# Four transformer layers on one core: token attention repacked into blocks of six heads

## The chip, the core and the metric

One core of a Trainium2 chip. The metric is device time in microseconds of the whole kernel. All tensors are float32. The engines are TensorE (PE in the profile, with its weight loads shown apart as PEld), VectorE (DVE), ScalarE (ACT), GpSimd (POOL) and SyncE (SP), which here does nothing but issue DMAs, in order.

## What is computed

The input is x of 4 sequences x 512 tokens x 288 channels and a condition vector per sequence. Four layers follow one another. Each has this shape (cut from the reference):

```python
shift1, scale1, gate1, shift2, scale2, gate2 = split(silu(c) @ w_ada + b_ada, 6)
h = layernorm(x) * (1 + scale1) + shift1
q, k, v = split_heads(h @ w_qkv + b_qkv)                 # 16 heads of 18
o = softmax(q @ k.T / sqrt(18)) @ v                      # over the 512 tokens of a sequence
x = x + gate1 * (o @ w_proj + b_proj)
h = layernorm(x) * (1 + scale2) + shift2
x = x + gate2 * mlp(h)                                   # 288 -> 1152 -> 288, gelu
```

Layers 0, 1 and 3 attend over tokens. Layer 2 attends, within each token, over its 16 heads. Layer 0's MLP is a mixture of four experts with the top two chosen per token.

## The kernel before, in words

The kernel is a single instruction stream per engine, whose order is made by a small scheduler at build time. The main loop of a stage emits its own matmuls and calls `gap(us)` between them (L139). Each call advances a counter `now` by one and lets `fill` (L120) emit pieces of waiting tasks into the gap: `products` (pieces with matmuls, as many as fit into `us` of estimated cost), `lanes` (DVE, ACT and POOL pieces), `loads` and `spreads` (DMAs). A task has a due gap, keys that must be marked ready, and a generator whose yields are estimated costs. A task that isn't due is taken only while the gap's allowance lasts; a due one is taken always. What a piece overshoots its allowance by is forgotten at the next gap. A mark (`mark`, L99) counts gaps, not time: the true waits are semaphores that the framework places between the instructions.

**Token attention (`attention`, L529).** A sequence b has four units of four heads; a unit takes four steps, one for each 128 rows of scores, so that a layer has 64 steps and six more ahead of them. In a step, `scores` (L648, called twice) multiplies, for the unit six steps ahead, queries by keys, whose row maxima DVE takes (L668), and for the present unit keys by queries, to which ACT applies exp (L661). `sum_values` (L683) then multiplies the exps of the step before by the values, which have a column of ones, so that the denominators come out as one more row. A head has 18 numbers and one more (`HO` is 19): the query's 19th holds the row maximum, the key's is -1, so that the maximum is subtracted within the matmul.

In the gaps of these steps lie, for each sequence:

- `chunks` (L493): the normed tokens are transposed and modulated, in three chunks of 96 channels. The third has a row of ones (97 rows), which brings the biases in.
- `queries_keys` (L578): 608 columns (4 units x 2 x 4 heads x 19) in five blocks of at most 128, with three matmuls of 512 columns for each (L562), copied by ACT (L587) into a ring of three tiles `qc`.
- `values` (L566): four tiles of tokens, three matmuls of 288 columns each (L562).
- `spread` (L592): one DMA per head and per query or key, two where a head straddles two blocks, moves 19 rows from `qc` to the unit's tile `qk`, where a head starts at row 0, 32, 64 or 96 (L606). These DMAs are issued by SP, and partly by ACT for the first unit.
- `set_maxima` (L672): four transposes (L676) of a unit's maxima, a copy by ACT (L678) and four DMAs (L680) into the 19th row of the queries.
- `denominators` and `normalise` (L701, L714): for each unit four transposes (L704) of the copied outputs (L698), a reciprocal (L706), a copy by POOL that repeats them over the head's 32 rows (L710), four transposes back (L717) and a multiplication by DVE (L720). All this stays within the engines.
- `project` (L724): four tiles, four matmuls of 288 columns (L727) each over a unit's 128 rows, most of which are padding; then the gate (L522) and the addition to x (L523).

`load_attention` (L228) loads the padded query and key weights of a layer: per unit, six DMAs of the weights (L248) and two of the biases (L252). `scale_queries` (L279) scales the query weights on POOL.

**Other stages.** Layer 0's expert MLP (`expert_block`, L1436) runs 19 blocks of 256 tokens. SP loads each block's tokens (L1382) and weights (L1397 to L1404), while the products of layer 1's first sequence, with their `spread` DMAs, already lie in its gaps. Its first four blocks are listed when two sequences are done; the others need all four. In layer 1 the MLP of sequence 0 is emitted within the attention's step 48 (`early_mlp`, L1813). Layer 2's attention over heads (`attention_over_heads`, L819) is a chain of DVE and POOL work beside layer 1's last MLPs; it writes its outputs to memory (`scratch`, L898) and reads them back (L902) through SP. Layer 3 is like the others, with a plain MLP at the end.

Of the kernel before, what the change touches and what calls it, by code (L numbers as in the profile page):

```python
# [16 lines left out]
NH, HD = 16, 18  # L17
# [23 lines left out]
UQ = 2 * HG * HO  # L41
NQ = NG * UQ
NQB = -(-NQ // P)
# [15 lines left out]
def tile_dit_blocks(ctx: ExitStack, tc: tile.TileContext, x_in, cond_t, sel_den, sel_b, w_gate, layers, out):  # L59
# [28 lines left out]
    flow = {"now": 0, "turn": 0, "others": (6, 7), "credit": 0.0, "rate": 0.0}  # L88
# [31 lines left out]
    def fill(where, started, us):  # L120

        while True:
            if not started:
                item = take(where, us <= 0)
                if item is None:
                    return
                started.append(item)
            if us <= 0 and started[0][0] > flow["now"]:
                return
# [5 lines left out]
            if took is WAIT:  # L135
                return
            us -= took

    def gap(us):  # L139
# [3 lines left out]
        fill(products, open_product, 0.0 if wanted else us)  # L143
# [57 lines left out]
    selb = const.tile([P, B, P], F32, name="selb")  # L201
# [9 lines left out]
    mxs = [const.tile([P, TB, HG], F32, name=f"mx{i}") for i in range(2)]  # L211


    spreads_of = [const.tile([P, 2, S], F32, name=f"qk{i}") for i in range(4)]

    def clear():
        for t in spreads_of:
            nc.gpsimd.memset(t, 0.0)
        mark("cleared")
        yield 0.5  # L220
# [5 lines left out]
    w_att = {l: {} for l in range(n_layers)}  # L226

    def load_attention(l):  # L228

        w, t = layers[l], w_att[l]  # L230

        wqk = wpool.tile([P, NK, NQ + C], F32, tag="wqk", name=f"wqk{l}")
        if l == OVER_HEADS:
            wqk = t["wqkv"] = wqk[:, :, : 3 * C]
            nc.sync.dma_start(wqk[:KP], w["wqkv"].rearrange("(k p) f -> p k f", p=KP))
            nc.sync.dma_start(wqk[KP : KP + 1, NK - 1, :], w["bqkv"])
        else:

            src = w["wqk"].rearrange("(k p) s (h d) -> p k s h d", p=KP, d=HP)
            bias = w["bqk"].rearrange("(o j d) s g -> o s g j d", o=1, d=HP)  # L240
            t["wqk"] = wqk[:, :, :NQ]
            wv = t["wv"] = wqk[:, :, NQ:]

            def load_unit(g, queue):
                for s in range(2):
                    at = slice(g * UQ + s * HG * HO, g * UQ + (s + 1) * HG * HO)
                    for k in range(NK):
                        queue.dma_start(  # L248
                            wqk[:KP, k, at].rearrange("p (j d) -> p j d", d=HO),
                            src[:, k, s, g * HG : (g + 1) * HG, :HO],  # L250
                        )
                    queue.dma_start(  # L252
                        wqk[KP : KP + 1, NK - 1, at].rearrange("p (j d) -> p j d", d=HO), bias[:, s, g, :, :HO]
                    )
                if g == 0:
                    queue.dma_start(wv[:KP], w["wv"].rearrange("(k p) f -> p k f", p=KP))
                    queue.dma_start(wv[KP : KP + 1, NK - 1, :], w["bv"])
                mark(("loaded", l, g), 6)

            t["load unit"] = load_unit  # L260
            if l > 0:
                for g in range(NG):
                    load_unit(g, nc.sync)
# [3 lines left out]
    def load_projection(l):  # L267
        w, t = layers[l], w_att[l]
        wp = wpool.tile([P, NG, C], F32, tag="wp", name=f"wp{l}")
        t["wp"] = wp  # L270
        if l == OVER_HEADS:
            nc.sync.dma_start(wp[:KP, :NK, :], w["wp"].rearrange("(k p) f -> p k f", p=KP))
            nc.sync.dma_start(wp[KP : KP + 1, NK - 1, :], w["bp"])
        else:
            nc.sync.dma_start(wp, w["wp"].rearrange("(g p) f -> p g f", p=P))
# [3 lines left out]
    def scale_queries(l, g):  # L279

        at = slice(g * UQ, g * UQ + HG * HO)
        for k in range(NK):
            q = w_att[l]["wqk"][: KP + (1 if k == NK - 1 else 0), k, at]
            nc.gpsimd.tensor_scalar_mul(q, q, SCALE)  # L284
        mark(("weights", l, g))
# [62 lines left out]
    def mod_product(l, half, kinds):  # L348
# [13 lines left out]
        for kind in kinds:  # L362
            at = slice(kind * HP, kind * HP + B)
            nc.vector.tensor_tensor(row[at, :C], pr[at, :C], bada[at, :], ALU.add)
            if kind < 2 and half == 1 and l:
# [8 lines left out]
    def modulation(l, half, kinds=range(3)):  # L374
# [6 lines left out]
        if half == 0:  # L381
# [5 lines left out]
        if half == 0:  # L387
# [1553 lines left out]
```

## Time and profile before

| what | value |
|---|---|
| time, median of 3 runs | 2488.81 us (2487.93 to 2495.96) |
| time of the profiled execution | 2477.4 us, of which the span of its instructions is 2475.6 us |
| token attention, layers 0, 1, 3 | about 45 to 472, 916 to 1354, 1936 to 2304 us of the span |
| expert MLP of layer 0 | about 472 to 916 us |
| attention over heads beside layer 1's MLPs | about 1354 to 1761 us |
| MLP of layer 2; MLP of layer 3 | about 1761 to 1936; 2304 to 2476 us |
| PE clock granted, mean | 0.941 of full |
| DMAs `qk<-qc` and `qk<-maxima` on SP | 417 and 192 |

The page gives busy time by engine, then the span in 40 slices of 61.9 us, each digit a tenth. A float32 matmul stands in the records as two instructions, a transpose as one; so the page's x384 for L727 are 192 matmuls (a few records are missing). A matmul's end is modelled, and one overlaps the next, so that busy times of lines add up to somewhat more than the time they take. Idle time of an engine is put down to what released it.

### The profile page before, as it was taken

The numbers are of one execution on the slowest core, as the hardware profiler recorded it, in microseconds if no ns is written. First come the engines' busy times: TensorE is split into PE (matmuls) and PEld (weight loads), VectorE is DVE, ScalarE is ACT, GpSimd is POOL, SyncE is SP. The second block draws the span as 40 slices with busy tenths as digits, with TensorE's granted clock in tenths as the row PEclk, the third lists the DMA queues.
The fourth block names the chain that finished last, engine by engine and source line by source line (L and its number), as shares of the span: only waits on it lengthen the run. The fifth ranks groups of instructions, "written<-read, shape, count | busy, mean of one in ns | idle before, by whom it ended". The sixth has DMA issues, their size and how long they took to land. (4 is left out here: it accounts for less than half of the span.)

```text
span 2475.6 us, 30149 instructions
## 1 busy us (share of the span) xinstructions
PE 2278.4 (92%) x11188; PEld 1211.7 (49%) x11188; DVE 1087.1 (44%) x1955; ACT 833.6 (34%) x1233; POOL 527.8 (21%) x544
## 2 busy tenths in 40 slices
PE   5999999799998999999998999778599999999998
PEld 2333333367775763333353676455467433333455
DVE  3556656240021124655434768989210445555100
ACT  1344444232222223444335233323223244444311
POOL 2000022130121110110010357778721000001000
PEclk7899999899999998999999999788799799999999
DMA  3211120366644540000000001111210100000000
GB/s 81 97 58 39 51 86 29 96 201 183 188 136 149 181 141 20 12 16 14 26 21 1 22 5 45 21 17 17 24 55 1 28 16 16 14 13 7 1 20 20
DMA packets 163033, 134.23 MB, mean 54 GB/s; under 512 B 81365, under 2 KB 146725, under 8 KB 162886
## 3 DMA queue, kind: packets, MB, share of 16 engines
q1 hardware_dynamic: 159520, 122.39, 17.0%
q0 software_dynamic: 3072, 9.44, 1.2%
q8 instruction: 89, 1.46, 0.2%
q14 instruction: 58, 0.48, 0.1%
q10 hardware_dynamic: 294, 0.47, 0.1%
HBM read 90.67 MB, written 26.25 MB: 47 GB/s over the span
## 5 line engine op out<-in xcount | busy, mean ns | idle before, releaser
L668 DVE TENSOR_REDUCE mx<-banks 128x1 f32<-128x512 f32 x696 | 448.0, 686 | 356.8 <-PE banks L616 356.2
L616 PE MATMUL banks<-qk 32*128 32x512 f32 x3072 | 537.1, 669 | 24.6 <-DMA qk<-qc 13.4
L661 ACT ACTIVATE ex<-banks 128x1024 f32<-128x1024 f32 x348 | 356.4, 1024 | 495.2 <-PE banks L616 493.0
L616 PEld LDWEIGHTS banks<-qk 32*128 32x128 f32 x3072 | 174.5, 191 | 238.4 <-DVE mx L668 97.2
L873 POOL TENSOR_TENSOR pv<-hs,qk 128x1152 f32<-128x1152 f32 x64 | 203.8, 3195 | 50.6 <-DVE ho L885 35.7
L690 PE MATMUL banks<-ex,va 128*32 128x512 f32 x1536 | 210.5, 619 | 0.0
L562 PE MATMUL banks<-ht,wqk 96*128 96x512 f32 (+1 forms) x360 | 189.7, 634 | 1.4 <-POOL wqk L284 0.8
L1472 PE MATMUL banks<-w_b,hid_b 128*128 128x288 f32 x684 | 187.8, 417 | 0.0
L1660 PE MATMUL banks<-ht,w 128*128 128x256 f32 x504 | 135.9, 406 | 36.0 <-ACT hid L1671 35.5
L1452 PE MATMUL banks<-block,w_b 128*128 128x256 f32 x684 | 164.4, 385 | 2.7 <-DMA w_b<-in_w 2.0
L710 POOL COPY rec<-r 128x512 f32<-128x512 f32 x48 | 29.5, 615 | 635.9 <-DVE r L706 562.2
L1682 PE MATMUL banks<-w,hid 128*128 128x288 f32 x504 | 155.6, 446 | 0.0
L1464 ACT ACTIVATE hid_b<-banks,b_b 128x256 f32<-128x256 f32 x171 | 68.7, 473 | 240.3 <-PE banks L1458 167.5
L1472 PEld LDWEIGHTS banks<-w_b,hid_b 128*128 128x128 f32 x684 | 124.0, 190 | 51.5 <-issue 23.1
L1452 PEld LDWEIGHTS banks<-block,w_b 128*128 128x128 f32 x684 | 128.8, 193 | 28.4 <-issue 7.8
L1660 PEld LDWEIGHTS banks<-ht,w 128*128 128x128 f32 x504 | 99.8, 203 | 60.4 <-ACT hid L1671 40.1
L727 PE MATMUL banks<-wp,ot 128*128 128x288 f32 x384 | 117.4, 431 | 5.9 <-DVE upd_a L522 3.5
L1682 PEld LDWEIGHTS banks<-w,hid 128*128 128x128 f32 x504 | 95.7, 202 | 48.0 <-issue 26.6
L523 POOL TENSOR_TENSOR x<-x,upd_a 128x288 f32<-128x288 f32 x48 | 38.0, 791 | 360.5 <-DVE upd_a L522 337.9
L562 PEld LDWEIGHTS banks<-ht,wqk 96*128 96x128 f32 (+1 forms) x360 | 61.2, 191 | 101.7 <-issue 87.8
L727 PEld LDWEIGHTS banks<-wp,ot 128*128 128x128 f32 x384 | 67.6, 192 | 74.9 <-issue 51.2
L690 PEld LDWEIGHTS banks<-ex,va 128*32 128x32 f32 x1536 | 30.9, 109 | 149.4 <-issue 147.7
(224 smaller groups left out, 2577.8 us busy)
## 6 DMA issues: line engine op xcount, KB each, us to landing
w_b<-in_w SPq DMA_DIRECT2D x57, 432.0 KB
w_b<-in_w SPq DMA_DIRECT2D x57, 384.0 KB
qk<-qc SPq DMA_DIRECT2D x327, 38.0 KB
wa<-in_wada SPq DMA_DIRECT2D x7, 864.0 KB
block<-x_mem SPq DMA_DIRECT2D x19, 288.0 KB
y_mem<-y_b SPq DMA_DIRECT2D x19, 288.0 KB
x_mem<-zeros SPq DMA_DIRECT2D x7, 768.0 KB
y_mem<-zeros SPq DMA_DIRECT2D x7, 768.0 KB
```

The source lines that it names most:

```text
L562: nc.tensor.matmul(to, st(rows, k), mv(rows, k), start=k == 0, stop=k == NK - 1)
L616: nc.tensor.matmul(to, qk[u][r, of, c * P : (c + 1) * P], qk[u][r, 1 - of, :], start=True, stop=True)
L661: nc.scalar.activation(e, WEIGHTS, AF.Exp)
L668: nc.vector.tensor_reduce(mxs[mu % 2][:, mc, h : h + 1], pm[j], AX.X, ALU.max)
L690: nc.tensor.matmul(SUMS[j * HP : (j + 1) * HP, :], vas[0][:, c, at : at + HP], ex[step, j // 2][:, j % 2, :], start=c == 0, stop=c == TB - 1,)
L727: nc.tensor.matmul(pp, done[b * NG + g][:, t * P : (t + 1) * P], w["wp"][:, g, :], start=g == 0, stop=g == NG - 1)
L873: nc.gpsimd.tensor_tensor(prod, sc[i][:, hs, :].unsqueeze(2).to_broadcast([P, GH, HD, NH]), qkv[i][:, 1].rearrange("p h d -> p d h").unsqu ...
L1452: nc.tensor.matmul(banks[:, UP + j, :BT], w1[:, k, j * P : (j + 1) * P], hx[i][:, k, :], start=k == 0, stop=False)
L1464: nc.scalar.activation(t, banks[:, UP + j, :BT], AF.Gelu_apprx_tanh, bias=b1[:, f : f + 1])
L1472: nc.tensor.matmul(banks[:, PY + t, :C], hid[j][:, t * P : (t + 1) * P], w2[:, j, :], start=f == 0, stop=f == NF - 1)
L1660: nc.tensor.matmul(banks[:, UP + j, :BT], full[:, k, (f % 3) * P : (f % 3 + 1) * P], h[:, k, s], start=k == 0, stop=False,)
L1682: nc.tensor.matmul(banks[:, PY + t, :C], hf[:, t * P : (t + 1) * P], w["w2"][f // 3][:, f % 3, :], start=False, stop=f == NF - 1,)
```

## The change

Layer 2 keeps its layout. In layers 0, 1 and 3:

- **Blocks.** Queries and keys are made in three blocks of six, six and four heads. A block fills two PSUM banks, one with queries and one with keys. Channels are cut as 128, 128 and 32; the 32 are stored repeatedly, at rows 0, 32 and 64, so that the last matmuls of two products can use different rows of the array. Biases leave the matmul: ACT adds them (and scales the queries) in the copy out of PSUM, DVE adds the values' bias. `scale_queries` becomes `scale_biases`, three small POOL instructions.
- **Spread.** One DMA per head carries queries and keys.
- **Maxima.** One transpose instead of four.
- **Outputs.** `gather_heads` packs a unit's outputs by five DMAs from SP into three tiles of 108, 90 and 90 rows, with the denominators beside them. The reciprocals are taken once for a sequence (eight transposes in all), written to memory with each row repeated 18 times, read back, and multiplied in by POOL. `project` takes three matmuls for a tile. The ring `ot` goes from seven tiles to four.
- **Loads.** Weights come in six DMAs for the layer, biases and projection rows are first packed in memory and then read; `selb` is no longer loaded. The zeros of the expert memory are written through POOL's queue.
- **Account.** Within the steps, what a gap's pieces overshoot or leave of their allowance is carried to the next (between -4 and 2), and the second allowance of a step goes from 1.0 to 1.4.
- The hidden tiles of the MLPs move from `ot` to `ex` (layer 1's and 2's halves stay in `ot`, two to a tile); `early_mlp` goes by two instead of three.

```diff
-UQ = 2 * HG * HO
+BLOCKS = ((0, 6), (6, 12), (12, 16))
+HEADS = ((0, 6), (6, 11), (11, 16))
...
         wanted = any(item[1] for item in chain)
-        fill(products, open_product, 0.0 if wanted else us)
+        if flow["even"]:
+            us = min(flow["room"] + us, 2.0)
+        flow["room"] = max(fill(products, open_product, 0.0 if wanted else us), -4.0)
...
+        for s in range(2):
+            for k in range(KF):
+                nc.sync.dma_start(
+                    full[:, k, s, :].rearrange("p (h d) -> p h d", d=HO), src[k * P : (k + 1) * P, s, :, :HO]
+                )
+            nc.sync.dma_start(
+                rest[s * RC : (s + 1) * RC].rearrange("p (h d) -> p h d", d=HO), src[KF * P :, s, :, :HO]
+            )
+        for g in range(NG):
+            nc.sync.dma_start(
+                packed_biases[l, g], w["bqk"].rearrange("(j d) s g -> g j d s", d=HP)[g, :, :HO, :]
+            )
+        rows = packed_biases[l].rearrange("g j d s -> (g j d) s")
+        for i, (h0, h1) in enumerate(BLOCKS):
+            nc.sync.dma_start(bqk[: (h1 - h0) * HO, :, i], rows[h0 * HO : h1 * HO, :])
...
-        PACE = (0.3, 1.0)
+        PACE = (0.3, 1.4)
...
+            to = [other()[:n, :] for _ in range(2)]
+            for s in range(2):
+                for k in range(KF):
+                    nc.tensor.matmul(to[s], w["full"][:, k, s, at], h[:, k, :], start=k == 0, stop=False)
+                    yield 0.86
+            for s in range(2):
+                r = slice(s * RC, (s + 1) * RC)
+                nc.tensor.matmul(to[s], w["rest"][r, at], h[r, KF, :], start=False, stop=True)
+            t = packed[b, i] = work.tile([P, 2, S], F32, tag="qc", bufs=2, name=f"qc_{l}_{b}_{i}")
+            for s in range(2):
+                nc.scalar.activation(
+                    t[:n, s, :], to[s], AF.Identity, bias=w["bqk"][:n, s, i : i + 1], scale=SCALE if s == 0 else 1.0
+                )
...
-                        queue = nc.scalar if u == 0 and j >= HG // 2 else nc.sync
-                        queue.dma_start(t[to : to + n, s, :], packed[b, m][r : r + n, :])
+                nc.sync.dma_start(t[j * HP : j * HP + HO], packed[b, i][r : r + HO])
...
-            for c in range(TB):
-                nc.tensor.transpose(pm[:HG, c * P : (c + 1) * P], mxs[u % 2][:, c], ident)
+            nc.tensor.transpose(pm[:n, :P], mxs[u % 2].rearrange("p j c -> p (j c)"), ident)
...
+        def gather_heads(u):
...
+            at = KP + 1 + g * HG
+            nc.sync.dma_start(last[at : at + HG, :], done[u][ONE::HP, :])
+            for j in range(HG):
+                k = [i for i in range(NK) if HEADS[i][0] <= g * HG + j < HEADS[i][1]][0]
+                at = (g * HG + j - HEADS[k][0]) * HD
+                nc.sync.dma_start(oc[b][k][at : at + HD, :], done[u][j * HP : j * HP + HD, :])
...
+        def normalise(b):
+            rows = dram.tile([NH, HD, S], F32, tag="rec", name=f"rec_rows_{l}_{b}")
+            nc.sync.dma_start(rows, rec[b][1 : 1 + NH, :].unsqueeze(1).to_broadcast([NH, HD, S]))
+            rows = rows.rearrange("h d s -> (h d) s")
...
+                    nc.sync.dma_start(room[k], rows[r0:r1, :])
+                for _ in range(3):
+                    yield WAIT
+                for k in ks:
...
+                    nc.gpsimd.tensor_tensor(oc[b][k][:n, :], oc[b][k][:n, :], room[k], ALU.mult)
+            mark(("outputs", l, b), 3)
...
-                    products, at_step(last if b + 1 == B else last + (7 if l == 0 else 11) + t),
-                    [("outputs", l, b * NG + g) for g in range(NG)] + [("gate", l, 0), ("projection", l)], project(b, t),
+                    products, at_step(last + 8 + 2 * t), [("outputs", l, b), ("gate", l, 0), ("projection", l)], project(b, t)
```

## The prediction

> **What bounds the kernel now.** I read the page's busy times and slices first, then the stretches of single stages, then TensorE's groups within layer 3's attention, its waits over the whole run, and SP's timeline where TensorE waited for a DMA.
>
> ```profile
> span 2475.6 us, 30149 instructions
> ...
> PE   5999999799998999999998999778599999999998
> ...
> PEclk7899999899999998999999999788799799999999
> ```
>
> TensorE is busy in nine tenths of most slices, and the clock falls where it was idle. The stretches (PE, PEld, DVE, ACT, POOL busy, clock) of layer 3's attention, of the attention over heads, and of one piece of the expert MLP:
>
> ```profile
> 2050.00:2100.00 50.00, 49.39 (x290) 17.61 (x292) 26.25 (x45) 22.06 (x25) 4.09 (x6) 1.00 0.05 17
> ...
> 1350.00:1750.00 400.00, 346.49 (x1428) 244.05 (x1424) 314.96 (x337) 120.42 (x228) 260.59 (x158) 0.88 0.10 20
> 735.00:785.00 50.00, 38.96 (x163) 26.93 (x162) 10.33 (x23) 8.20 (x20) 14.56 (x14) 0.90 0.43 131
> ```
>
> Token attention is TensorE's: 49.39 of 50 us, with DVE at 53%. The attention over heads is a chain of DVE (315 of 400 us) and POOL, so TensorE work saved there gives nothing. TensorE's groups from 2000 to 2290 us, where 13 units (3.25 sequences) pass:
>
> ```profile
> L616 PE MATMUL banks<-qk 32*128 32x512 f32 x824 | 125.6, 639 | 0.2 <-ACT ex L643 0.2
> L690 PE MATMUL banks<-ex,va 128*32 128x512 f32 x416 | 55.4, 605 | 0.0
> L562 PE MATMUL banks<-ht,wqk 96*128 96x512 f32 (+3 forms) x72 | 37.5, 625 | 0.0
> L727 PE MATMUL banks<-wp,ot 128*128 128x288 f32 x96 | 31.2, 435 | 1.3 <-DVE upd_a L522 1.2
> L562 PE MATMUL banks<-wqk,ht 96*128 96x288 f32 (+1 forms) x72 | 22.7, 433 | 1.2 <-DVE va L572 1.2
> L676 PE MATMUL banks<-ident,mx 128*4 128x128 f32 x52 | 8.7, 272 | 3.2 <-DVE mx L668 3.2
> L717 PE MATMUL banks<-ident,rec 128*128 128x128 f32 x52 | 8.3, 282 | 0.0
> L704 PE MATMUL banks<-ident,ot 128*128 128x128 f32 x52 | 8.2, 281 | 2.2 <-ACT ot L698 2.2
> ```
>
> Idle before these is 8 us of 290. With 5.6 us for the transposes of L508 they sum to 303 us, so a busy us stands for 0.93 us of time (282/303). TensorE's DMA waits over the run, and SP's queue at one of them:
>
> ```profile
> PE banks L1425 <- DMA block<-x_mem: 20.6, 3, 9.0
> PE banks L915 <- DMA rows<-scratch: 18.7, 1, 18.7
> ...
> PE banks L616 <- DMA qk<-qc: 13.4, 2, 12.4
> ```
>
> ```profile
> 735.30 19.89 SPq L606 DMA_DIRECT2D qk<-qc  x18
> ...
> 758.19 11.59 SPq L606 DMA_DIRECT2D qk<-qc  x9
> ```
>
> SP issues one after the other; 27 spread DMAs at 0.6 to 1.3 us hold back an expert block's tokens and weights, and TensorE stands at 759 us.
>
> **The change part by part.** *TensorE, for a sequence.* From the groups: a query or key matmul takes 37.5/36 = 1.04 us, a values one 0.63, a projection one 0.65, a transpose 0.16 to 0.17.
>
> Before: queries and keys 15 x 1.04 = 15.6; values 12 x 0.63 = 7.6; projection 16 x 0.65 = 10.4; maxima 16 x 0.17 = 2.7; denominators and back 32 x 0.16 = 5.1. Sum 41.4.
>
> After: queries and keys 12 x 1.04 = 12.5, and three pairs of 32-row remainders. Nearest row: L1604 does three such remainders at once, 17.0 us for 15 triples, 1.1 us; three pairs 3.3. Values 8 x 0.63 and two pairs at 0.7 (L1667's pairs of 256 columns take 0.63 from their start to the next matmul's): 6.4. Projection 12 x 0.65 = 7.8; maxima 4 x 0.17 = 0.7; reciprocals 8 x 0.16 = 1.3. Sum 32.0.
>
> The difference is 9.4 busy us, 8.7 us of time; for 12 sequences 105 us. Could it be less? The Trainium skill (Perfetto Trace Analysis, Identifying the Most-Contended Engine) says that matmul busy share doesn't show how full TensorE is, and to go by weight-load share: here 17.6/50 = 35%. By that rule TensorE has room and the saving is near 0. But in this window something follows each matmul at once, and neither DVE nor ACT is over 55%; I go by the gaps, not by the modelled ends. A step is 5.6 us now and would be 5.1. The exp chain sets a floor: two score rounds of 1.1 us, each followed by an exp of 1.02 before its banks are free, 4.4 us a step. Steps that get few pieces come near it and lose part of the gain. I take 80%: **-84 us** (bounds -52 and -105).
>
> *DVE and ACT.* DVE loses 48 multiplications of 0.69 us, ACT gets six biased copies of 0.77 (row L509) for five of 0.59 a sequence: both are off the path, hidden by TensorE; uncovered, ACT's would cost 12 x 1.7 = 20 us. POOL gets three multiplications of some 1.25 us (between L523's 0.79 for 288 columns and L1694's 1.40 for 576) a sequence and loses four copies of 0.61: hidden, at 7% busy.
>
> *SP.* A unit's spread falls from about nine DMAs to four, the gather adds five, the maxima stay four: 13 either way, about 8 of 22 us. But what is moved matters. In the expert MLP the spreads become 12 instead of 27: the 11 us of idle around 759 and half of the 10 us at half clock behind it should go. Loads of a layer shrink from 34 DMAs to some 17, so that L915 (18.7 us behind 23 us of loads) gains 6 to 8, and layer 1's load before the expert MLP about 4. The start (12.4 us for the first `qk<-qc`) may gain 3, less what the packed biases' two trips take. **-25 us** (-10 to -35).
>
> *New waits.* (a) Reciprocals go through memory: SP writes 590 KB, waits for it to land, then reads. The row: `rows<-scratch`, the same size, took 4.4 us from issue (1794.08) to the transposes it releases (1798.50): 8.8 for both ways. The skill (DMA: Bandwidth & Descriptors, Anatomy of one DMA) gives 2.0 us fixed plus bytes at 436 GB/s, 6.7 for both, and says that a wait on memory can be surprisingly long. I take the row; no one needs the projection for some steps, so TensorE waits 0. What is queued behind SP in that time is a `set_maxima` or a `spread`: 0 to 4 us a sequence. (b) `set_maxima` may be emitted a gap later. Now the ACT copy L678 starts 6.3 to 14 us, mostly over 10, before the copy L698 of the unit before, and that stands about 2 us behind the scores that read the row: 4.3 to 12 us are there. Four issues of 0.54 (L680) and the same page's 2.0 us of landing need 4.2. A gap is 2.6 us; the tight units would stall 1 to 2 us. Both: **+8** (0 to 40). (c) A pair holds both free banks (6 and 7), so a pair right behind another waits for ACT, up to 1.5 us, five a sequence: **+8** (0 to 30). (d) Layer 0's last sequence: its outputs come some 30 gaps of 1.2 us behind the attention instead of 13 us. Block 4 of the experts was loaded at 554 us and used at 576, so that 18 us were spare: **+11** (0 to 25) with the slow clock behind the stall. Layer 3's last sequence has 111 us of MLPs ahead of it, and needs about 90: 0 (to 15). The account, the rings, POOL's zeros and the early MLP by two (two more remainder groups at some 1 us): 0 to 2, I take 0; bounds -5 and +5.
>
> Sum: -84 - 25 + 27 = -82 on 2477.4, the profiled execution's own time (span 2475.6): 2395. The median of the runs is 0.46% above that execution: **2406 us**.
>
> **The rivals.**
>
> *All of it arrives.* The account keeps all steps even: -105 - 35 + 10 = -130, 2347, as a median 2358. For it: idle is so small now. Against: the exp floor.
>
> *Half is eaten.* Late maxima and paired banks cost what the upper bounds allow, the exp floor takes half: -52 - 10 + 40 = -22, as a median 2466.
>
> *SP becomes the pacemaker.* The normalisation, now free of DMAs, hangs on 20 gathers a sequence; SP stands at each new sequence until the tiles `oc` are free, and the four maxima DMAs of each unit stand behind. If the first weights of each of 48 units then wait 3.5 us, that is 168 us, over twice the saving: +86, as a median 2575. It decides from 82/48 = 1.7 us a unit. For it: the expert MLP shows just this blocking, and a 3.3 us gap at 996 us was followed by 10 us at half clock. Against: `qk<-maxima` cost TensorE 1.0 us in all before, with as many DMAs.
>
> **How the numbers follow.** The main case 0.45 (2375 to 2445), all arrives 0.22, half eaten 0.13, SP 0.20. About 0.3% is what a measurement of this kernel can tell from no change. Half eaten gives 0.08 to faster and 0.05 to the same: faster 0.75, same 0.05, slower 0.20. The range, 2335 to 2515, holds all but the SP case and a thin tail below.
>
> **What would show it.** The three attentions should be 25 to 35 us shorter each, with L727 at x288 and L676 at x48. The stand at 759 should be gone, L915's wait shorter, a new stand at the experts' block 4. If TensorE shows waits for the maxima's DMA at many units, or slices of attention below 9, the SP case holds. I am wrong also if the steps stay at 5.6 us though TensorE has less to do.

## The result, and the profile after

The changed kernel takes 2566.81 us (median of 4 runs, 2562.18 to 2571.13) beside 2488.37 us before: a ratio of 1.033, 95% interval 1.030 to 1.0359. It is slower. I had predicted 2406 us, in a range of 2335 to 2515. The profiled execution:

```profile
span 2565.3 us, 28976 instructions
...
PE   6899989589996999989999999869669999999998
...
PEclk9799999789998997998999989879789899999999
```

The page counts 10732 matmul records on PE where there were 11188, and yet more slices lie below 9. By stage (columns: PE, PEld, DVE, ACT, POOL busy, clock granted, DMA share, GB/s), for the start to attention 0's end, the experts, attention 1, attention over heads with MLPs, attention 3. Before:

```profile
45.20:445.90 400.70, 385.44 (x2156) 141.77 (x2156) 232.58 (x492) 171.73 (x209) 42.70 (x69) 0.96 0.17 58
445.90:916.00 470.10, 443.27 (x2104) 318.23 (x2096) 81.19 (x253) 111.90 (x246) 72.05 (x95) 0.96 0.52 159
916.00:1348.30 432.30, 409.59 (x2192) 163.44 (x2194) 212.29 (x389) 176.38 (x207) 42.49 (x56) 0.95 0.08 24
1348.30:1935.80 587.50, 505.58 (x2062) 351.13 (x2056) 331.48 (x377) 172.21 (x326) 310.19 (x221) 0.88 0.12 25
1935.80:2301.00 365.20, 351.55 (x2006) 130.95 (x2006) 199.77 (x357) 165.82 (x192) 27.29 (x40) 0.96 0.04 11
```

After:

```profile
50.60:475.00 424.40, 390.79 (x1996) 145.92 (x1998) 224.97 (x477) 171.27 (x217) 56.61 (x83) 0.94 0.21 67
475.00:980.30 505.30, 446.41 (x2112) 320.00 (x2104) 80.04 (x252) 114.20 (x251) 73.20 (x92) 0.93 0.50 152
980.30:1434.30 454.00, 423.52 (x2032) 162.63 (x2032) 200.92 (x362) 174.57 (x212) 47.01 (x54) 0.92 0.13 36
1434.30:2024.50 590.20, 501.35 (x2070) 344.14 (x2066) 327.76 (x376) 174.86 (x330) 310.75 (x215) 0.89 0.13 27
2024.50:2389.80 365.30, 351.81 (x1844) 133.37 (x1844) 188.32 (x330) 162.13 (x195) 32.03 (x38) 0.95 0.10 27
```

The loss is +24 us in attention 0, +35 in the experts, +22 in attention 1, +5 at the start, and nothing in attention 3. But attention 3 has 162 records fewer and didn't gain either; PE is as *busy* as before. The granted clock is lower as well: at 0.95 in place of 0.92 attention 1 would take 454.0 x 0.92/0.95 = 440 us, by an estimate that lets its whole time go with the clock.

These stages are from one profile each. Attention 0 took 401 us at a clock of 0.96 here, and 416 us at 0.93 in v1_before_later (below), which is the same program up to 430 us. So of the +24 up to 15 us may be the clock of that one execution. (The changed kernel's attention 0 took 425 us in two profiles; attention 3 takes 365 to 367 us in the profiles of before, v1 and y4.) TensorE's groups in 290 us of layer 3's attention (to be read beside those of before):

```profile
L635 PE MATMUL banks<-qk 32*128 32x512 f32 x810 | 156.7, 641 | 3.8 <-DMA qk<-tops 3.8
L712 PE MATMUL banks<-ex,va 128*32 128x512 f32 x408 | 55.5, 617 | 0.0
L603 PE MATMUL banks<-ht,wqk 128*114 128x512 f32 (+1 forms) x56 | 30.8, 654 | 0.7 <-DVE upd_a L538 0.6
L791 PE MATMUL banks<-wp,oc 108*128 108x288 f32 (+2 forms) x72 | 21.0, 424 | 0.0
L580 PE MATMUL banks<-wqk,ht 128*128 128x288 f32 x48 | 13.5, 421 | 0.0
...
L695 PE MATMUL banks<-ident,mx 128*16 128x128 f32 x13 | 3.6, 277 | 4.1 <-DVE va L586 2.5 <-ACT qc L610 0.8 <-ACT ht L525 0.8
```

The products shrank as worked out. The scores, untouched by the change, went from 125.6 us for 824 records to 156.7 for 810, with the same mean of one. That is the main reading of this case: a wait hidden in busy time. For all three attentions, the time from each matmul's start to the next one's, added up by kind (us; "sums" are the exps times the values, "other products" all else that TensorE does there):

| kernel | scores | sums | other products | the three attentions |
|---|---|---|---|---|
| before | 515 | 204 | 481 | 1198 |
| after | 657 | 196 | 391 | 1244 |
| after, rows cut at 16 (below) | 627 | 194 | 374 | 1196 |

The other products and sums fell by 98 us, and the scores took 142 more. TensorE's waits:

```profile
PE banks L748 <- DMA oc<-ot: 30.0, 3, 29.3
PE banks L635 <- DMA qk<-tops: 23.7, 13, 7.0
PE banks L973 <- DMA rows<-scratch: 22.9, 2, 20.7
...
PE banks L1483 <- DMA block<-x_mem: 14.6, 2, 14.1
...
PE banks L1510 <- DMA w_b<-in_w: 7.5, 1, 7.5
```

Three things, each followed below: the last gathers of layer 0 (29.3 us once), the maxima rows (`qk<-tops`, 1.0 us before), and the wait for `rows<-scratch` behind layer 3's load, no shorter than before.

### The profile page after: what moved, and what is told of

It is laid out like the page before. It is cut to its first block, busy times and chain, and to the rows that moved or that the text cites. A ratio compares the mean times of both kernels' runs of the same rounds, so it can differ in the third digit from the quotient of the medians.

```text
span 2565.3 us, 28976 instructions
## 1 busy us (share of the span) xinstructions
PE 2305.9 (90%) x10732; PEld 1213.0 (47%) x10732; DVE 1048.0 (41%) x1871; ACT 833.3 (32%) x1257; POOL 551.0 (21%) x536
## 4 chain that ended last, share of the span: by engine, by line
PE 71%; DMA 8%; DVE 7%; POOL 6%; SPq 3%; ACT 2%; issue 2%; POOLq 0%; DVEq 0%; ACTq 0%
PE banks L635 22%; PE banks L712 7%; PE banks L1532 6%; PE banks L1510 5%; PE banks L603 4%; POOL pv L931 4%; PE banks L1686 3%; PE banks L1657 3%; PE banks L791 3%; PE banks L1747 3%; PE banks L1723 2%; DMA qk<-tops 2%; PE banks L580 2%; DVE hs L921 1%; PE banks L1516 1%
## 5 line engine op out<-in xcount | busy, mean ns | idle before, releaser
L635 PE MATMUL banks<-qk 32*128 32x512 f32 x3072 | 652.4, 674 | 34.8 <-DMA qk<-tops 23.7
L635 PEld LDWEIGHTS banks<-qk 32*128 32x128 f32 x3072 | 243.6, 194 | 348.4 <-issue 135.1
L712 PE MATMUL banks<-ex,va 128*32 128x512 f32 x1536 | 216.1, 633 | 0.2 <-ACT ex L662 0.2
L783 POOL TENSOR_TENSOR oc<-oc,by 90x512 f32<-90x512 f32 (+1 forms) x36 | 45.1, 1265 | 751.2 <-DMA by<-rec_rows 736.9
L603 PE MATMUL banks<-ht,wqk 128*114 128x512 f32 (+1 forms) x288 | 153.9, 650 | 5.0 <-ACT qc L610 4.3
L1747 PE MATMUL banks<-w,hid 128*128 128x288 f32 x504 | 148.9, 431 | 0.0
L458 DVE BATCH_NORM_STATS2 st<-x 128x6 f32<-128x288 f32 x128 | 56.0, 438 | 116.3 <-POOL x L1760 84.1
L915 DVE TENSOR_TENSOR pq<-banks,qk 128x1152 f32<-128x1152 f32 x64 | 86.2, 1347 | 37.5 <-issue 21.0
L1569 POOL DMA_INDIRECT outs<-y_mem,places x32 | 30.8, 963 | 309.2 <-DMA w_b<-in_w 122.8
L791 PE MATMUL banks<-wp,oc 97*128 97x288 f32 (+2 forms) x288 | 90.6, 441 | 7.3 <-POOL oc L783 4.1
```

What stands on the lines that cost most here:

```text
L603: nc.tensor.matmul(to[s], w["full"][:, k, s, at], h[:, k, :], start=k == 0, stop=False)
L635: nc.tensor.matmul(to, qk[u][r, of, c * P : (c + 1) * P], qk[u][r, 1 - of, :], start=True, stop=True)
L712: nc.tensor.matmul(SUMS[j * HP : (j + 1) * HP, :], vas[0][:, c, at : at + HP], ex[step, j // 2][:, j % 2, :], start=c == 0, stop=c == TB - 1,)
L791: nc.tensor.matmul(pp, oc[b][k][:n, t * P : (t + 1) * P], w["wp"][:n, k, :], start=k == 0, stop=k == NK - 1)
L915: nc.vector.tensor_tensor(prod, QUERIES[i % 2][:, :C].rearrange("p (h d) -> p h d", d=HD)[:, hs, :].unsqueeze(2).to_broadcast([P, GH, NH, ...
L1747: nc.tensor.matmul(banks[:, PY + t, :C], hf[:, t * P : (t + 1) * P], w["w2"][f // 3][:, f % 3, :], start=False, stop=f == NF - 1,)
```

## Experiments

My theory after the result: (A) the maxima rows are late because of one DMA engine; (B) the pieces lie unevenly, so that rounds of scores (a round is the four score matmuls of one call of `scores`) wait; (C) at layer 0's end the gathers stand on SP behind a load. The rival was the recorded one: SP as the pacemaker. Ratios are to the kernel before, on the same chip; the stages are from one profile each.

**The transfers of 19 rows (A).** One maxima row late, in layer 3:

```profile
2191.73 2.63 SPq L699 DMA_DIRECT2D qk<-tops  x4
...
2196.78 1.13 PE L635 MATMUL banks<-qk 32*128 32x512 f32 x4
...
2200.40 2.16 PE L635 MATMUL banks<-qk 32*128 32x512 f32 x4 [2.49 <-DMA qk<-tops]
```

The DMA records of that time (us, packets begun in that microsecond, their mean ns):

```
2193.0 512B x6(25) 4096B x6(160)
2194.0 512B x3(26) 4096B x6(160)
2195.0 512B x3(25) 2048B x3(82) 4096B x7(161)
...
2199.0 512B x4(27) 2048B x5(84) 4096B x1(159)
```

A spread DMA (19 rows of 4096 B) runs packet behind packet, six a microsecond, which is 1000/160: one at a time. The last four packets of the maxima came only when that stream ended. The Trainium skill (DMA: Bandwidth & Descriptors, "Why a DMA increments its semaphore by 16 and not by 1") says that a DMA uses the largest number of engines up to 16 that divides the slowest dimension of both its source and its target; 19 is prime, so by that rule one. Sixteen rows would use sixteen.

x1_spray:

```diff
-                nc.sync.dma_start(t[j * HP : j * HP + HO], packed[b, i][r : r + HO])
+                nc.sync.dma_start(t[j * HP : j * HP + 16], packed[b, i][r : r + 16])
+                nc.sync.dma_start(t[j * HP + 16 : j * HP + HO], packed[b, i][r + 16 : r + HO])
```

> The changed kernel, with each of a unit's four spread transfers (19 rows of 4096 B) cut into 16 rows and 3 rows. Theory A (one DMA engine): the 19 rows run packet behind packet on a single engine, 159 ns each, and the fourth maxima row (qk<-tops) stands behind them; cut in 16 rows they go to 16 engines. Then the waits of the scores for qk<-tops (23.7 us, 13 times) fall below 5 us, with the slow clock behind them, and SP is held less in the experts: 2527 to 2547. Theory B (the matmul pieces lie unevenly, the maxima rows matter little): 2560 to 2570. Against both: SP issues four more DMAs a unit at 0.5 us; if SP is the pacemaker, 2575 or more.

1.0068 (1.0047 to 1.009), 2496.47 us: some 65 us gained by the ratios, more than expected. The packets agree: in the changed kernel more than one packet of 4096 B was under way in only 13 of the 624 us in which any was; with the rows cut up to 13 were, and the same packets needed 211 us in all. From the start of the last issue of a unit's maxima to the end of their last packet it took 1.31 us in the median and 7.34 at worst; with the rows cut, 1.31 and 2.78. Of the wait 4.6 us are left:

```profile
PE banks L636 <- DMA qk<-tops: 4.6, 8, 0.6
```

SP issues four DMAs more a unit and the kernel is faster, so SP's issuing is not the pacemaker. Attention 0 got 28 us shorter, attention 1 11, attention 3 9, the experts 26.

r1_tops_queue left the spreads alone and moved the maxima rows:

```diff
-                nc.sync.dma_start(
+                nc.scalar.dma_start(
                     qk[u][j * HP + ONE : j * HP + ONE + 1, 0, :].rearrange("o (c q) -> o c q", c=TB),
```

> The changed kernel as it is, with the four maxima rows of a unit (qk<-tops) issued from ACT's queue in place of SP's. If the rows were late because they stood on SP's queue (its issues, or its packets ahead of theirs on the one DMA engine), the waits for qk<-tops fall from 23.7 us to under 8 and the attentions give 20 to 35 us: ratio 1.017 to 1.024; the expert stage stays long. If the engine itself, shared by the queues, is what holds them, or if the 64 us were SP held by full queues, 1.028 to 1.034.

1.0662 (1.0633 to 1.0691), 2651.04 us: neither. The wait stayed, and a new one came:

```profile
PE banks L635 <- DMA qk<-tops: 25.4, 9, 4.8
...
PE banks L635 <- ACT ex L680: 24.3, 21, 1.9
```

In 11 of 48 units (6 in the changed kernel) the rows still landed over 2 us after the start of their last issue, and in each of the 11 between 23 and 29 packets of 4096 B began in that time. That fits what the same page says ("Issuing engines are not separate DMA queues"): DMAs of all issuing engines run on the same 16 DMA engines and interleave. The trace doesn't name the engine of a packet. Four issues at 0.58 us on ACT now stand ahead of exps, and the attentions take 30, 20 and 25 us more. So delaying ACT delays the kernel; that it is the exps is tested below.

y4_before_spray, in the kernel before:

```diff
-                        queue.dma_start(t[to : to + n, s, :], packed[b, m][r : r + n, :])
+                        for a0, a1 in ((0, min(n, 16)), (16, n)):
+                            if a0 < a1:
+                                queue.dma_start(t[to + a0 : to + a1, s, :], packed[b, m][r + a0 : r + a1, :])
```

> The kernel before with each of its spread transfers cut at 16 rows. If the single DMA engine became a cost only with the packets of 4096 B and with one transfer for queries and keys, it gains nothing here and pays 9 more issues a unit: 1.000 to 1.010. If it held the kernel before as well, 0.985 to 0.995, and the 64 us are not a cost of the change.

0.9999 (0.9988 to 1.001). Its packets are 2048 B at 84 ns in the median, and they too ran one at a time for 535 of 592 us; there it cost nothing. The 65 us belong to the change.

**Layer 1's load (C).** SP at layer 0's end, where TensorE stands 29.3 us from 486 on:

```profile
490.39 3.05 SPq L258 DMA_DIRECT2D wqk<-in_wqk  x2
...
497.84 2.79 SPq L265 DMA_DIRECT2D packed_biases<-in_bqk  x4
507.18 2.98 SPq L270 DMA_DIRECT2D bqk<-packed_biases  x3
...
512.17 0.60 SPq L735 DMA_DIRECT2D oc<-ot  x1
512.81 3.06 SPq L739 DMA_DIRECT2D oc<-ot  x4
```

The last unit's gathers are issued at 512, behind the experts' blocks and behind layer 1's load, whose biases SP waits to see land in memory (501 to 507).

x3_load_later, for layers 1 and 3:

```diff
-            task(loads, at_step(-LEAD) - 20, [("first products", prev, B - 1), ("all made", prev)], load_attention(l))
+            task(loads, at_step(-LEAD) - 20, [("first products", prev, B - 1), ("all made", prev)] + [("x", prev, 1, B - 1)], load_attention(l))
```

> The changed kernel, with layer 1's attention weights loaded only after layer 0's last projection, so that the gathers of the last unit do not stand behind them on SP. Theory: the 29.3 us stand for oc<-ot at 486 shrinks to under 10, with the 34 us at half the clock behind it: 2530 to 2545. Rival: the gathers stand behind the experts' blocks and weights anyway, or the load now comes late for attention 1: 2555 to 2570.

1.0207 (1.0174 to 1.024), 2533.35 us. The wait shrank as expected:

```profile
PE banks L748 <- DMA oc<-ot: 7.7, 3, 7.0
```

But the number was met by luck: most of the 33 us (590 to 565) came ahead of layer 3, where `rows<-scratch` no longer stands behind that layer's load. The experts' stretch fell by only 11 us, and the wait for `w_b` rose from 7.5 to 16.4. Nor does the slow clock lie behind the stand, as my expectation has it: in the changed kernel's trace the granted clock was 0.51 in the 30 us of the stand (486 to 516), 0.75 in the next 10 and 0.86 in the 24 after these. v1_before_later made the same edit in the kernel before.

> The kernel before with the loads of layers 1 and 3 behind the last projection of the layer ahead. In the changed kernel with the rows cut this edit also took the 25 us stand for rows<-scratch ahead of layer 3 away (593 to 569 us between the attentions). If that stand was a cost of the kernel before as well, 15 to 25 us: 0.990 to 0.994, and only 10 of the 36 us of that edit belong to the change. If the 34 transfers come too late for layer 3's first scores, 1.000 or more.

0.9871 (0.9825 to 0.9917), more than expected: the stretch ahead of layer 3 went from 587 to 559 us and the wait for `rows<-scratch` fell to 2.7 us. This stand was never the change's cost, nor could halving the number of DMAs cure it: the order does. y1_spray_later joined both edits.

> The changed kernel with the spreads cut in 16 and 3 rows and layer 1's load behind layer 0's last projection. If the two are separate costs (one DMA engine; SP's order at layer 0's end) their gains add: 64 + 28 us off, a ratio to the kernel before of 0.993 to 1.000. If both removed the same waits of the expert stage, 1.003 to 1.007.

0.9891 (0.9865 to 0.9917), 2460.16 us: the two gains add, to somewhat more than expected.

**Uneven pieces (B).** x2_no_account:

```diff
-                flow["even"] = 0 <= step < N_STEPS - LEAD
+                flow["even"] = False
```

> The changed kernel without the running account (each gap takes pieces up to 0.3 and 1.4 of its own again, as before the change with 0.3 and 1.0). Theory B (the account leaves rounds of scores with nothing between them, which then stand for the exp and the maxima: 3.6 instead of 2.14 us for two): those pairs fall from about 20 to under 8 in layer 3's 300 us, the three attentions are 10 to 20 us shorter each, 2510 to 2540. Theory A (DMA rows late): the same within 10 us, 2557 to 2577, since the waits for qk<-tops stay.

1.023 (1.0201 to 1.0259), 2539.07 us: within theory B's range, but not for B's reason. Rounds at once (two with nothing between them) did not become fewer in layer 3 (29 against 24). The waits for `qk<-tops` fell from 23.7 to 9.9 us, so a part of the account's cost was that it sent the maxima late. y2_all_three is y1 without the account.

> As the one before, and without the running account. If the account leaves rounds of scores without work between them, another 15 to 20 us: 0.985 to 0.993. If its loss was only that it sent the maxima rows late into a busy DMA engine, nothing is left of it once the rows are cut: within 0.003 of the run with the two edits.

0.9839 (0.9805 to 0.9873), 2448.99 us: 11 us faster than y1, less than theory B's 15 to 20, with intervals that overlap. Whether the account costs anything beyond the late rows isn't shown.

x4_before_less takes TensorE work out of the kernel *before*, in `project`:

```diff
-            for g in range(NG):
+            for g in (0, NG - 1):
```

> The kernel before, with two of the four head groups left out of the projection after token attention (the output lacks them): 8 matmuls of 0.65 us a sequence, 62 busy us in all, taken away with nothing put in their place. The prediction's price (0.93 us of time for a busy us, 80% of it arriving) gives 46 us: 2442. The rival, that a matmul taken out of a step comes back as a wait for the exp and maxima at the scores, gives under 20: 2468 or more.

0.9871 (0.9846 to 0.9896), 2448.91 beside 2480.25: 31 of 62 us. Half of a saved busy us arrives, with no change to any DMA; within attention 3's stretch it was 1 us of 14. What do the rounds wait for? Two rounds with nothing between them, in the changed kernel:

```profile
2107.99 1.01 ACT L680 ACTIVATE ex<-banks 128x1024 f32<-128x1024 f32 x1
2108.59 3.87 PE L635 MATMUL banks<-qk 32*128 32x512 f32 x16
...
2110.26 1.02 ACT L680 ACTIVATE ex<-banks 128x1024 f32<-128x1024 f32 x1 [0.78 <-PE banks L635]
...
2111.34 0.30 PEld L635 LDWEIGHTS banks<-qk 32*128 32x128 f32 x4 [0.55 <-ACT ex L680]
2112.39 1.07 PE L712 MATMUL banks<-ex,va 128*32 128x512 f32 x8
2112.57 1.02 ACT L680 ACTIVATE ex<-banks 128x1024 f32<-128x1024 f32 x1 [1.29 <-PE banks L635]
```

The second exp starts 2.31 us after the first: 1.02 of exp, then 1.29 in which the next two scores, whose weight load waited for it, run and their result reaches ACT. Ordered by what lay between, rounds in 330 us of layer 3's attention (1960 to 2290 before, 2050 to 2380 after):

| other work between two rounds | rounds before | after | round takes |
|---|---|---|---|
| none (two at once) | 6 | 21 | 3.6 us for both |
| under 1.2 us | 5 | 26 | 1.3 to 1.9 us, mostly; with the filling 2.3 to 2.4 |
| over 1.2 us | 98 | 38 | 1.1 us |

(14 stretches of scores in after were broken up by other products and are not counted.) In layer 3's rounds no exp starts within 2.25 us of the one before it, in either kernel; half of them start within 2.31 after the change, within 2.75 before it. A round's four scores read different rows (a head's tile rows start at 0, 32, 64 and 96) and together take 1.07 us. The last two of the second round above waited for the exp and ran alone from 2111.34 to 2112.39: 1.05 us, as long as four. That is how waiting becomes busy time.

Which chain is this? y3_exp_halves cut each exp in two, w1_half_reduce halved DVE's reduces, r2_both_halves did both, all on y1:

```diff
-                nc.scalar.activation(e, WEIGHTS, AF.Exp)
+                for j in range(2):
+                    nc.scalar.activation(e[:, j], WEIGHTS[:, j], AF.Exp)
...
-                    nc.vector.tensor_reduce(mxs[mu % 2][:, h, mc : mc + 1], pm[j], AX.X, ALU.max)
+                    nc.vector.tensor_reduce(mxs[mu % 2][:, h, mc : mc + 1], pm[j][:, : S // 2], AX.X, ALU.max)
```

> As the run with the two edits, and each exp of two banks (1.02 us) cut into two of one bank, so that the next round's first scores wait for the first half alone. If the exp behind a round of scores is the floor that ate the saved matmuls, two rounds that follow at once take about 3.0 instead of 3.6 us and the three attentions get 5 to 12 us shorter each: 0.982 to 0.992. If the rounds wait for the maxima's banks (DVE) or the pieces, no change, or some us slower from ACT's extra instructions: 0.996 to 1.004.

> The run with two edits (rows cut at 16, layer 1's load later), with each reduce of maxima over half of its columns (the shift of the softmax is then a maximum over half the keys). A round of scores never follows the one before it in under 2.3 us. If the two reduces of 0.65 us that free the maxima's banks set this, two rounds at once take under 3.3 instead of 3.6 us, and the time falls by 10 to 25 us, to 0.979 to 0.985. If the exp sets it, 3.5 us or more stay and the time is within 6 us of that run: 0.987 to 0.992.

> The run with two edits, with both: each exp in two halves, and each reduce over half its columns (the shift is a maximum over half the keys). If exp and reduce are two chains of about the same length that each hold a round to 2.3 us, two rounds at once fall from 3.6 to under 3.0 us and the time by 15 us or more: under 0.983. If something else sets the round (the latency between engines, the order of TensorE's queue), it stays within 0.986 to 0.992.

0.9903 (0.9872 to 0.9934), 0.99 (0.9867 to 0.9933) and 0.9862 (0.9831 to 0.9893): no change beyond the interval against 0.9891. DVE is not the chain. And y3 was a bad test: its half exps take 0.60 us each, so that two end no earlier than one whole of 1.02, and the second bank's scores wait for that. s2_half_exp, also on y1, does the exp on half its columns, and the sums read these twice:

```diff
-                nc.scalar.activation(e, WEIGHTS, AF.Exp)
+                nc.scalar.activation(e[:, :, : S // 2], WEIGHTS[:, :, : S // 2], AF.Exp)
```

> The run with two edits, with each exp over half its columns and the sums reading these twice (the other half of the queries is left out). If scores (1.07 us) and the exp behind them (1.02) are the chain that holds a round to 2.3 us, two rounds at once fall from 3.6 to 3.0 to 3.2 us, the attentions get 8 to 20 us shorter each and the ratio is 0.965 to 0.981. If not, 0.986 to 0.991.

0.9726 (0.9686 to 0.9765), 2409.71 us, some 41 us below y1 by the ratios. The attentions got 15, 19 and 20 us shorter, all of it in the scores (628 us in y1, 574 here; sums and other products within 1 us), and two rounds at once take 3.13 us on average. The exps:

```profile
2010.84 3.06 PE L636 MATMUL banks<-qk 32*128 32x512 f32 x16
...
2012.13 0.60 ACT L681 ACTIVATE ex<-banks 128x512 f32<-128x512 f32 x1 [0.56 <-PE banks L636]
...
2014.02 0.60 ACT L681 ACTIVATE ex<-banks 128x512 f32<-128x512 f32 x1 [1.30 <-PE banks L636]
```

1.89 in place of 2.31 us from exp to exp, and the difference is the exp's own 0.42. Scores, exp, scores on one pair of banks is the chain. How much of the 112 us that the scores take beyond 515 with the rows cut it explains isn't measured: taking 0.42 us out of each exp gave 54 back.

Can the gaps be filled better? w2_split_even (on y1) and w3_split_no_account (on y2) put two of the four sums behind each round, with `PACE` at 0.85 and 0.6 for both gaps:

```diff
                     scores(step, 0)
-                    sum_values(step - 1)
+                    sum_values(step - 1, range(0, 2))
...
                     scores(step, 1)
+                    sum_values(step - 1, range(2, 4))
```

> The run with two edits, with the four sums of a step divided, two behind each round of scores, and the account given 0.85 for both gaps. If the saved matmuls were lost because one gap of a step held over 2 us of other work and the other under 1.2 (a round then waits and its four scores no longer run side by side), rounds under 1.2 us of filling fall from about 60 of 130 to under 30 in layer 3 and the attentions get 8 to 25 us shorter each: 0.962 to 0.981. If a chain of ACT and DVE sets the step, not how the gaps are filled, within 0.003 of that run's 0.989.

> The run with three edits, with the sums divided in the same way and 0.6 for both gaps, no account. By the same reasons 0.965 to 0.979; if filling does not matter, 0.981 to 0.987. If the account is what keeps the pieces even, it is slower than the run with the account and divided sums.

1.0201 (1.0156 to 1.0245) and 1.0225 (1.0183 to 1.0266): far slower, and for a reason that I had not thought of. In w2 layer 3's scores fell from 202 to 180 us and almost no two rounds came at once, but the sums rose from 63 to 118. Half the sums take as long as all:

```profile
2100.86 1.05 PE L713 MATMUL banks<-ex,va 128*32 128x512 f32 x4
...
2103.11 1.05 PE L713 MATMUL banks<-ex,va 128*32 128x512 f32 x4
```

(x8 in 1.07 above). The Trainium skill (TensorEngine Tiling (Array Packing), Key Properties) says that different tiles of the array can run matmuls in parallel; the four sums write to four strips of 32 rows, and I had cut them apart.

r3_second_gap (on y1) keeps the pieces for the gap that has no sums, with `PACE` at 0.3 and 1.7:

```diff
+        if flow["even"] and us == 0:
+            flow["room"] = max(flow["room"] + fill(products, open_product, 0.0), -4.0)
+        else:
+            if flow["even"]:
+                us = max(min(flow["room"] + us, 2.0), 0.1)
...
-                    gap(PACE[0])
+                    gap(0.0)
                     scores(step, 1)
```

> The run with two edits, with the account changed: the gap with the sums takes only what is late, the gap without them takes the step's 1.7 and at least one piece. If gaps with under 1.2 us of other work are where the saved matmuls go, rounds at once (two with nothing between) fall from 24 to under 10 in each attention and it gains 15 to 35 us: 0.975 to 0.983. If pieces are simply not there when a gap needs them (all that is ready has been taken), 0.986 to 0.991.

0.9839 (0.9812 to 0.9866), 2445.86 us, between the two forecasts, with an interval that just overlaps y1's: rounds at once went from 24 to 17 in layer 3, not under 10. Attention 0 gained 13 us, attention 1 9, attention 3 nothing.

**What the outputs' packing is worth.** r4_old_outputs is y2 with `denominators`, `normalise`, `project` and `load_projection` as before the change.

> The run with three edits, with the outputs handled as before the change (denominators and normalisation by transposes for each unit, projection over four groups of heads; no gathers, no reciprocals through memory), the queries' and keys' packing kept. By the prediction's prices the outputs' packing saves 6.4 of the 9.4 us a sequence, so undoing it costs 60 us: about 1.008. If the saved matmuls fill gaps that would be waits, and the gathers cost DMA and SP time, it costs under 15 us or gains: 0.975 to 0.990.

0.9957 (0.9941 to 0.9973), 2479.14 us: 29 us slower than y2, in between, and made of two parts. The attentions take 411 + 447 + 379 in place of 385 + 430 + 359 us: the outputs' packing is worth some 62 us there, nearly the 60 of the expectation. In these stretches it takes 69 us of other products and 25 of sums away, and 33 come back in the scores (436, 217 and 584 us here; 367, 192 and 617 in y2). But the experts' stretch takes 445 us in place of 478, with the clock at 0.99 in place of 0.96:

```profile
463.40:908.50 445.10, 437.40 (x2116) 315.94 (x2108) 80.88 (x253) 113.81 (x249) 70.25 (x89) 0.99 0.55 162
```

So 33 us are given back right behind layer 0's attention, where the last sequence's outputs now go a longer way. s1_last_queues, on r3, at layer 0's end:

```diff
+            queue = nc.scalar if (l, u) == (0, N_UNITS - 1) else nc.sync
+            queue.dma_start(last[at : at + HG, :], done[u][ONE::HP, :])
...
+            queue = nc.gpsimd if (l, b) == (0, B - 1) else nc.sync
+            queue.dma_start(rows, rec[b][1 : 1 + NH, :].unsqueeze(1).to_broadcast([NH, HD, S]))
```

> The run with the second gap filled first, and at layer 0's end the last unit's five gathers issued by ACT and the last sequence's four transfers of reciprocals by POOL. If the stretch from the first to the second attention is 33 us longer than with the old outputs because these stand on SP behind the experts' blocks and weights, it falls from 478 by 8 to 20 us: 0.976 to 0.981. If the way itself is too long (gather, transposes, two trips through memory, multiplication), by under 4 us: 0.982 to 0.986.

0.985 (0.9806 to 0.9894): the stretch fell by 6 us and the total didn't move. SP's order is then at most a small part of the 33; the way itself was not shortened in any run, so what in it costs most stays open.

r4 also shows what the rest of the change is worth. It keeps the blocks of six heads with their spread, and its attentions take some 19 us more than v1's 415, 436 and 366: 5 less in attention 0, 11 more in attention 1 and 13 more in attention 3. Against v1 50 us of other products are gone, but 56 came into the scores and 12 into the sums (v1: 486, 206 and 527 us).

## Why the prediction failed, by its own steps

- **TensorE's work, -9.4 busy us a sequence, 105 us in all.** Nearly right: 98 us by the table. None of it comes from the query and key products, which my own sums had at 15.8 after 15.6; in layer 3's 290 us they measure 38.2 (L603 and L607) after 37.5.
- **80% of it arrives (-84).** This is the step that failed, and most of the 161 us by which I missed: the attentions got 45 us longer. In the changed kernel nothing arrived, because the scores took 142 us more. 30 of these are the late maxima rows (627 with the rows cut); 112 stayed, and s2 shows the chain through the exp in them. I had the floor nearly right, 4.4 us a step where two rounds measure 4.6 (my own figures, 2 x (1.1 + 1.02), give 4.2), and used it wrongly: I set a mean step of 5.1 against it. It holds for each gap: one has the sums (1.07 us, just under the 1.2 that a round needs), the other has pieces or none. Even in the kernel before only half of a saved us arrives (x4). One share for all was wrong too: with the rest mended the outputs' part arrived nearly as priced (62 us in the attentions, r4), while the blocks' part, priced at some 27 us (3.0 x 0.93 x 0.8 for 12 sequences), cost 19. The rule of the Trainium skill on weight loads (Perfetto Trace Analysis, Identifying the Most-Contended Engine), from which I drew a saving near 0, and which I weighed and set aside, was nearer for layer 3 (366 us before and after, 359 in y2) than my row of gaps.
- **DVE, ACT and POOL hidden.** Not quite for ACT: 13 of the 384 exps start right behind a pair of the new biased copies (1.26 us a pair; 22 exps in r4, none before), so up to 16 us may stand there. No run isolates it. And ACT's exp was the pacer, which I called only a floor.
- **SP, -25.** Wrong in sign: the start got 5 us longer, and L915's 18.7 us became 20.7 (L973); v1 shows that the order, not the number of DMAs, makes this wait. The stand at 759 came back as 7.5 us for `w_b` and 14.1 for `block<-x_mem` at 802 and 817, and went with the rows cut (1.4 us for `block<-x_mem` in x1). SP itself was held: between 770 and 819 us six of its issues took 2.6 to 6.8 us each, three of them spreads; with the rows cut none in the experts took 2 us.
- **(a) Reciprocals through memory.** Nearly right for TensorE, which waited 4.1 us for POOL's products. SP waited 6.7 us a sequence for the landing of the write (80.8 in 12), where I had 4.4. (The skill's 2.0 us, which I used here and in (b), stand in a section of DMA: Bandwidth & Descriptors, Anatomy of one DMA, that is on DMAs which GpSimd issues; these are issued by SP.)
- **(b) Late maxima, +8 with (a), at most 40.** The mechanism was right, the size wrong: its term rested on issue and landing times and left out what lies ahead on the DMA engine. Cutting the rows gave 65 us, all stages together, where I had at most 40 for (a) and (b).
- **(c) Paired banks, +8.** No run isolates it. It is one candidate for what the blocks cost in r4; ACT's pairs of copies, the changed spread, the maxima's single transpose and `PACE` are others.
- **(d) Layer 0's last sequence, +11 (to 25).** 29.3 us at once. I looked for it at block 4; it came ahead, at the gathers, which I had not placed in SP's queue behind layer 1's load. Mending that order took 22 us off this wait and only 11 off the stretch (x3), so SP's order is a part of the 35 us lost there. Cutting the rows took 26 us off it (x1); how the two share the loss is open.
- **The rivals.** SP as pacemaker, 2575, is near in number and wrong in cause: more issues on SP made the kernel faster (x1), and moving the maxima off SP did not shorten their wait (r1). What fits is an exp chain, one DMA engine and a bad place in SP's order.

The account with the ratios: after 1.033; rows cut 1.0068; load later as well 0.9891; no account, or the second gap first, 0.9839. Of these the load order, 1.3%, was to be had before the change (v1, 0.9871), so the mended packing beats that by 0.3% with overlapping intervals: it is not shown to be worth anything.

## What to carry to other kernels

Price a saved microsecond at the place where it is saved: if the engine's other work fills the shadow of a chain (here scores, exp, scores: 2.3 us a round), a part of the saving comes back as waiting (half in x4, none in attention 3), and a busy engine with no idle doesn't prove that it is the bound. Before merging transfers, see how many of their packets run at once, and what must land behind them. When work is handed to an in-order queue, list what stands ahead of its last, not its mean, instance.

## What the runs showed of the hardware

- DMAs of 19 rows moved their packets one at a time (4096 B, 159 ns each); cut in 16 and 3 up to 13 ran at once, 4.6 of 23.7 us of waiting were left, and 4 more issues a unit cost less than the spreading gave. Small rows behind such a stream came no earlier on a second queue (late in 11 of 48 units, in 6 on the same queue).
- Four float32 matmuls of 512 columns over four groups of 32 rows, or into four groups of 32 columns, take 1.07 us, two take 1.05: dividing such a set nearly doubled its price (63 to 118 us in layer 3).
- A matmul that starts late beside its three neighbours shows as busy, not idle: the same scores took 142 us more, and the profile's idle before them in layer 3 was 3.8 us.
